# Attention: bias add, row statistics and reciprocals used at later steps, send casts chained to each other

## The chip, the cores and the metric

One NeuronCore of a Trainium2 chip runs the whole program. The metric is the device time of one execution in microseconds. One execution is also recorded by the hardware profiler; the times inside a profile are counted from the start of its span. TensorE (PE in the tables) multiplies matrices, VectorE (DVE), ScalarE (ACT) and GpSimd (POOL) do elementwise work, and SyncE (SP) issues most DMAs. Each engine works through its own queue in order.

## The reference

The network has two layers on an input x of shape 2 x 256 x 56 x 56 (batch, channels, height, width). The change lies in the first half of layer 0, local attention; the sends it speaks of feed the second half, a mixture of experts.

```python
# layer 0
x = x + L0_conv(ln_c(x))         # windowed attention, residual
t = to_tokens(x)
t = t + L0_ffn(ln_t(t))          # experts, top 2 of 8, residual
x = from_tokens(t, x)
# L0_conv: 8 heads of 32 channels, each query sees a 7 x 7 window
q, k, v = proj(x, wq, bq), proj(x, wk, bk), proj(x, wv, bv)
attn = softmax(einsum('bhdxy,bhdxyw->bhxyw', q, windows(k)) * scale)
out = proj(einsum('bhxyw,bhdxyw->bhdxy', attn, windows(v)), wo, bo)
# L0_ffn: logits = t @ router_w.T; softmax, top 2, weights normalised
out = t; for e in range(8): out += combine[:, e] * (gelu(t @ w1[e] + b1[e]) @ w2[e] + b2[e])
# layer 1: two ternary 3 x 3 convolutions with batch norm, then experts again
```

## The kernel before

**Strips and slots.** The image pair is cut into 14 strips of 8 rows (448 tokens, seven strips an image). The attention loop runs over the strips; each strip has 8 slots (4 windows of columns by 2 halves of the heads). In a slot, `scores` (L1485) computes the scores sc of one window on TensorE and their exponentials ex on ScalarE, and `attend` (L1518) takes the slot before: it multiplies ex by the values into av and adds av to the accumulator acc on VectorE (L1534). So in every slot 4 + 4 score products, 4 value products, 2 exponentials and 2 accumulations pass, and everything else of a strip is spread between them.

**Step by step helpers.** `project` and `leave` are generators: each `yield` ends a step. `project(g + 2)` runs one step a slot during strip g: row statistics of the input (`token_stats`, L709), the normalised rows xn on ScalarE (`scaled`, L735), their transposes (L1435), the k and q projections (L1447), the v projections (L1469). `leave(g - 1)` (L1539) begins once strip g's slots are written out, and `push` (L1618) advances each open generator one step a slot. Its steps in the kernel before:

1. `again` (L1376) loads the residual rows xr from memory on SP's queue (L1379) and adds the output bias bo to them (L1380) on GpSimd, or on VectorE for the last two strips; the sums of the softmax are stored (L1553) and come back as den (L1557).
2. nothing.
3. the reciprocal rden (L1560) is stored as shares (L1561) and comes back spread over partitions as rec (L1564); den is checked (L1570 to L1572).
4. nothing.
5. acc times rec gives oc (L1581), eight products on VectorE.
6. oc times wo gives pw on TensorE (L1594), added to xr (L1602).
7. `norm` (L766): row statistics of xr on VectorE (L714 to L719).
8. GpSimd turns them into t_rstd and t_nmr (L729 to L731); for the last two strips ScalarE and VectorE do it.
9. u, the normalised rows, on ScalarE (L737).
10. transposes of u (L784); u is added to xr (L791, GpSimd), which is stored as x_mid (L792).
11. the router's logits (L800, L811).
12. the strip is entered as routed.

When both strips of a pair are routed, `settle` (L814) follows: four steps find the top two experts and each token's place, and then comes one step for each of the 8 blocks of 112 tokens: a cast of the places to integers (L884, VectorE) and two sends, indirect DMAs from GpSimd that scatter rows of u to the experts' buffer xs (L888). The last two strips settle alone, 4 blocks each.

**Order.** In this stage a scheduler fixes each queue's order when the program is built: an instruction written earlier has precedence, but one that is ready in its model may pass others. `tc.issue_after(pace[-1])` (L883) keeps a cast behind the last accumulation of its slot; `attend` sets `pace` (L1537), and it is cleared after the loop (L1661). Inside the expert stage (`experts`, L1045) the order on SP, VectorE, TensorE and ScalarE is as written.

**End of the loop.** `plan_first` (L1626) plans the first 27 expert tiles as soon as strips 0 to 9 are counted (`FIRST`). After the loop the experts start: weights (L1097) and rows of xs (L1086) are loaded, rows are transposed (L1107), multiplied (L1139, L1158), and the results are scattered to ys from GpSimd (L1170). At each tile `beside` (L1730) pushes the leaves and settles that are still open; when none is left, `routed_all` (L1684) plans the other tiles and computes the gates, TensorE's product pf (L1695) among it.

Buffers: xr and xt have two each, oc and rec one, u four.

Of the kernel before, what the change touches and what calls it, by code (L numbers as in the profile page):

```python
# [66 lines left out]
FIRST = (10, 8)  # L67
# [13 lines left out]
def bcast(ap, axis, shape):  # L81
    return ap.unsqueeze(axis).to_broadcast(shape)
# [551 lines left out]
def metaformer(ctx: ExitStack, tc: tile.TileContext, a: dict, out: bass.AP, flag):  # L634
    nc = tc.nc
# [73 lines left out]
    def token_stats(tp, src, eps, root, paced=False):  # L709

        stats = tp.tile([TT, NTT, 6], F32, tag="t_stats", name="t_stats")
        mv = tp.tile([TT, NTT, 2], F32, tag="t_mv", name="t_mv", bufs=3)
        for t in range(NTT):
            nc.vector.bn_stats(stats[:, t, :], src[:, t, :])  # L714
        for t in range(NTT):
            nc.vector.bn_aggr(mv[:, t, :], stats[:, t, :])
        rstd = tp.tile([TT, NTT], F32, tag="t_rstd", name="t_rstd", bufs=3)
        nmr = tp.tile([TT, NTT], F32, tag="t_nmr", name="t_nmr", bufs=3)
        nc.vector.tensor_scalar_mul(nmr, mv[:, :, 0], -1.0)  # L719
        if paced:  # L720
            yield
        if root:
            nc.scalar.activation(rstd, mv[:, :, 1], AF.Sqrt, bias=eps[:TT])
        yield
        if root:
            nc.vector.reciprocal(rstd, rstd)
            nc.vector.tensor_tensor(nmr, nmr, rstd, ALU.mult)
        else:
            nc.gpsimd.tensor_tensor(rstd, mv[:, :, 1], eps[:TT].to_broadcast([TT, NTT]), ALU.add)  # L729
            nc.gpsimd.tensor_tensor(rstd, rstd, minus_half, ALU.pow)  # L730
            nc.gpsimd.tensor_tensor(nmr, nmr, rstd, ALU.mult)  # L731
            yield
        return rstd, nmr

    def scaled(dest, src, rstd, nmr):  # L735
# [9 lines left out]
    pace = []  # L745

    def routing(layer, wp, tp, ps):
# [66 lines left out]
        def settle(strips, paced=False):  # L814


            n = len(strips) * NTT
            t0 = strips[0] * NTT
            us = [rows.pop(i) for i in strips]
            full, row = [TT, n, E], (TT, n)  # L820

            def small(name, shape=(TT, n, E), dt=F32):
                return tp.tile(list(shape), dt, tag=f"{name}_{n}", name=name, bufs=1)

            def first_max(v, m, hot, at):

                nc.vector.tensor_reduce(m, v, AX.X, ALU.max)
                nc.vector.tensor_tensor(hot, v, bcast(m, 2, full), ALU.is_equal)
                nc.vector.tensor_tensor(hot, hot, bcast(order, 1, full), ALU.mult)
                nc.vector.tensor_reduce(at, hot, AX.X, ALU.min)  # L830
                nc.vector.tensor_tensor(
                    hot, bcast(order, 1, full), bcast(at, 2, full), ALU.is_equal
                )

            lg = lgs[:, t0 : t0 + n, :]
            m = [most[:, j, t0 : t0 + n] for j in range(TOP)]
            hot = small("hot", (TT, TOP, n, E))
            at = small("at", (TT, TOP, n))
            rest = small("rest")
            first_max(lg, m[0], hot[:, 0], at[:, 0])  # L840
            for q, u in enumerate(us):
                small_eng.tensor_copy(u[:, :, R_EX], at[:, 0, q * NTT : (q + 1) * NTT])
            nc.vector.scalar_tensor_tensor(rest, hot[:, 0], NEVER, lg, ALU.mult, ALU.add)
            yield
            first_max(rest, m[1], hot[:, 1], at[:, 1])
            yield

            hots = small("hots", dt=BF16)
            nc.vector.tensor_tensor(hots, hot[:, 0], hot[:, 1], ALU.add)
            seen_b = small("seen_b", (TT, E), BF16)  # L850
            nc.vector.tensor_copy(seen_b, seen)
            here = small("here", (TT, E))
            nc.vector.tensor_reduce(here, hots.rearrange("p n e -> p e n"), AX.X, ALU.add)
            nc.vector.tensor_tensor(seen, seen, here, ALU.add)
            if strips[-1] == FIRST[layer] - 1:
                nc.vector.tensor_copy(seen_b4, seen)
                counted.append(True)
            if paced:
                yield
            rk = ps.tile([TT, n, E], F32, tag="aux", name="rk")  # L860
            nc.tensor.matmul(rk, before_w, hots, start=True, stop=False)
            nc.tensor.matmul(rk, all_w[:, :TT], bcast(seen_b, 1, full), start=False, stop=n == 1)
            for t in range(n - 1):
                nc.tensor.matmul(
                    rk[:, t + 1 :, :],
                    all_w[:, :TT],
                    bcast(hots[:, t, :], 1, [TT, n - 1 - t, E]),
                    start=False,
                    stop=t == n - 2,
                )  # L870
            yield
            place = small("place")
            nc.vector.tensor_tensor(place, rk, bcast(base_t, 1, full), ALU.add)
            nc.vector.tensor_tensor(hot, hot, bcast(place, 1, [TT, TOP, n, E]), ALU.mult)
            rowf = small("rowf", (TT, TOP, n))
            nc.vector.tensor_reduce(rowf, hot, AX.X, ALU.add)
            if layer == 1:
                nc.vector.tensor_copy(pos[:, :, t0 : t0 + n], rowf)
            yield
            for t in range(n):  # L880
                if layer == 0:

                    with tc.issue_after(pace[-1]) if pace else nullcontext():  # L883
                        nc.vector.tensor_copy(  # L884
                            pos[:, :, t0 + t : t0 + t + 1], rowf[:, :, t : t + 1]
                        )
                for j in range(TOP):
                    w = nc.gpsimd.indirect_dma_start(  # L888
                        xs[:, :],
                        bass.IndirectOffsetOnAxis(ap=pos[:, j, t0 + t : t0 + t + 1], axis=0),  # L890
                        us[t // NTT][:, t % NTT, :],
                        None,
                    )
                    apart(f"rows{layer}", w)
                    if FIRST[layer] and strips[0] >= FIRST[layer]:

                        disjoint(w, f"late{layer}", f"early{layer}")
                yield
            sent.extend(strips)
# [453 lines left out]
    with ExitStack() as st:  # L1353
        aw = st.enter_context(tc.tile_pool(name="att_w", bufs=1, reuse_waits="tile"))
        tp = st.enter_context(tc.tile_pool(name="att_t", bufs=2, reuse_waits="tile"))
        ps = st.enter_context(tc.tile_pool(name="att_ps", bufs=2, space=PSUM, reuse_waits="tile"))
# [16 lines left out]
            xt[g] = sp.tile([TT, NTT, C], F32, tag="xt", name="xt")  # L1373
            nc.sync.dma_start(xt[g], a["x_tok"][g])

        def again(g, eng):  # L1376

            xr[g] = tp.tile([TT, NTT, C], F32, tag="xr", name="xr")
            nc.sync.dma_start(xr[g], a["x_tok"][g])  # L1379
            eng.tensor_tensor(xr[g], xr[g], bcast(bias["o"], 1, [TT, NTT, C]), ALU.add)  # L1380

        load(0)
# [37 lines left out]
            nc.gpsimd.memset(t[:, :, :, 1:3, :], 1.0)  # L1420
            vals.append(t)
        keys = {}
        norm0, settle0, tiles0, _, gates0, wgt0, counted0, _ = routing(0, aw, tp, ps)

        def project(g):
            s = g % NS
# [112 lines left out]
        def leave(g):  # L1539
# [2 lines left out]
            rows = slice(s * SR, (s + 1) * SR)  # L1542

            late = g >= len(STRIPS) - 2
            again(g, nc.vector if late else nc.gpsimd)


            sums = dram.tile([2, PAIRS * NT], F32, tag="sums", name="sums", bufs=2)
# [8 lines left out]
            nc.sync.dma_start(den, sums.rearrange("i (p n) -> (i p) n", n=DEN))  # L1557
            yield
            yield
            nc.vector.reciprocal(rden, den)  # L1560
            nc.sync.dma_start(shares.rearrange("i (p n) -> (i p) n", n=DEN), rden)  # L1561
            rec = tp.tile([P, PAIRS, NT], F32, tag="taken", name="rec", bufs=1)
# [7 lines left out]
            nc.vector.tensor_scalar(fit, den, LEAST, None, ALU.is_ge)  # L1570
            nc.vector.scalar_tensor_tensor(fit, den, MOST, fit, ALU.is_le, ALU.mult)
            nc.vector.tensor_tensor(fits, fits, fit, ALU.add)  # L1572
            yield
            yield
            oc = tp.tile([P, KC, NT], F32, tag="oc", name="oc", bufs=1)
# [48 lines left out]
        plans0, taken = [], []  # L1624

        def plan_first():  # L1626
            if counted0 and not plans0:
                plan, n = tiles0(0)
                plans0.append(plan)
                taken.append(n)  # L1630
# [7 lines left out]
        for g in range(len(STRIPS)):  # L1638
# [18 lines left out]
            if g % NS == NS - 1:  # L1657
                attend(*before)
                before = None
                under_way.append(later(4, leave(g)))  # L1660
        pace.clear()  # L1661
        loop.close()
        while not plans0:
            push()
            plan_first()


        tiles_on = ctx.enter_context(ExitStack())
# [81 lines left out]
    with mid:  # L1750

        with ExitStack() as st:
            rp = st.enter_context(tc.tile_pool(name="raw", bufs=1, reuse_waits="tile"))
            ps = st.enter_context(tc.tile_pool(name="conv_ps", bufs=4, space=PSUM, reuse_waits="tile"))
# [9 lines left out]
            tp = strips_on.enter_context(  # L1764
                tc.tile_pool(name="conv_t", bufs=2, side="right", reuse_waits="tile")
            )
# [320 lines left out]
        with ExitStack() as both:  # L2087
# [6 lines left out]
            tp = both.enter_context(  # L2094
                tc.tile_pool(name="route_t1", bufs=2, side="right", reuse_waits="tile")
            )
# [55 lines left out]
            norm, settle, tiles, planning, gates, wgt1, _, sent = routing(1, wp, tp, ps)  # L2152
# [259 lines left out]
```

## Time and profile before

| what | us |
|---|---|
| runs | 1847.08, 1842.25, 1848.16; median 1847.08 |
| the profiled execution, its own time | 1836.06 |
| its span | 1834.3 |
| attention, first accumulation to the last | 44.6 to 516.5 |
| first expert tile's transposes | 524.5 |
| last expert product of layer 0 | about 831 |

| engine | busy us | share of the span | instructions |
|---|---|---|---|
| TensorE, matmul | 1523.4 | 83% | 8612 |
| VectorE | 978.8 | 53% | 2690 |
| ScalarE | 701.5 | 38% | 1362 |
| GpSimd | 656.1 | 36% | 664 |

How to read it: a group of lines names line, engine, operation and tile, `out<-in`; a bracket at the end of a timeline row gives the idle time of the engine before that instruction and what ended it. `remote` and `issue` there mean that the profile shows no releaser. A matmul counts with its modelled end. The granted clock is the share of TensorE's full speed.

### The profile page before, as it was taken

To read this page: it belongs to the slowest core of one execution; us is meant where nothing else is said; L and a number is where in the kernel's file an instruction comes from. 1 tells how busy PE (TensorE), PEld (TensorE's weight loads), DVE (VectorE), ACT (ScalarE), POOL (GpSimd) and SP (SyncE) were. 2 spreads that over 40 slices of the span, in tenths; PEclk is the share of its full clock that TensorE was granted. 3 is DMA by queue.
4 is the path that set the end of the run, shared out by engine and by line. 5 is a ranking of instruction groups with operands and counts; after the bars stand their busy time and mean duration, and the time that the engine had idled before them with its cause. 6 is when DMAs were issued, how large, how long until landed. Compare 5 with 4: busy or idle time off the path is not lost. (4 is left out here: it accounts for less than half of the span.)

```text
span 1834.3 us, 25840 instructions
## 1 busy us (share of the span) xinstructions
PE 1523.4 (83%) x8612; PEld 1191.8 (65%) x8612; DVE 978.8 (53%) x2690; ACT 701.5 (38%) x1362; POOL 656.1 (36%) x664
## 2 busy tenths in 40 slices
PE   6999998899788858894899799666468799999964
PEld 3555565555466747782788687556457688988953
DVE  4467556476645336855999897675422211111137
ACT  3454433434333324643454443233243333333322
POOL 3012524335343663442244144154553322222210
PEclk9999988999888979996999899755579899999985
DMA  7022324212267757985652000033635568888858
GB/s 241 27 82 83 108 88 122 58 56 83 57 192 232 248 192 265 308 274 161 166 161 61 1 1 1 21 114 99 226 129 186 179 232 273 286 276 294 287 181 311
DMA packets 91886, 291.77 MB, mean 159 GB/s; under 512 B 20487, under 2 KB 35803, under 8 KB 80416
## 3 DMA queue, kind: packets, MB, share of 16 engines
q1 hardware_dynamic: 66736, 231.79, 39.8%
q0 software_dynamic: 21200, 51.82, 8.1%
q10 hardware_dynamic: 3808, 6.42, 1.0%
q8 instruction: 70, 1.15, 0.3%
q14 instruction: 72, 0.59, 0.1%
HBM read 218.51 MB, written 74.20 MB: 160 GB/s over the span
## 5 line engine op out<-in xcount | busy, mean ns | idle before, releaser
L1139 PE MATMUL ph<-ut,w 128*128 128x256 f32 (+1 forms) x1472 | 316.8, 366 | 32.7 <-ACT h L1146 27.5
L1158 PE MATMUL py<-w,h 128*128 128x256 f32 x1288 | 304.1, 385 | 0.0
L1139 PEld LDWEIGHTS ph<-ut,w 128*128 128x128 f32 x1472 | 255.1, 198 | 63.5 <-ACT h L1146 29.0
L1168 DVE TENSOR_TENSOR y<-py,w 128x512 f32<-128x512 f32 (+1 forms) x120 | 76.8, 640 | 409.6 <-PE py L1158 358.2
L888 POOL DMA_INDIRECT xs<-u,pos x224 | 218.1, 974 | 168.6 <-issue 84.4
L1158 PEld LDWEIGHTS py<-w,h 128*128 128x128 f32 x1288 | 247.4, 194 | 34.6 <-DVE y L1168 0.4
L1170 POOL DMA_INDIRECT ys<-y,dest x136 | 136.7, 1005 | 269.9 <-DVE dest L1114 161.0
L1146 ACT ACTIVATE h<-ph,w 128x256 f32<-128x256 f32 (+1 forms) x368 | 162.4, 448 | 115.6 <-PE ph L1139 84.4
L1514 ACT ACTIVATE ex<-sc 112x476 f32<-112x476 f32 (+3 forms) x224 | 117.0, 571 | 207.0 <-PE sc L1504 172.9
L1111 ACT COPY ut<-pt 128x512 f32<-128x512 f32 (+1 forms) x120 | 65.3, 544 | 320.0 <-PE pt L1107 234.2
L1524 PE MATMUL av<-ex,vals 112*64 112x238 f32 (+3 forms) x896 | 125.9, 403 | 16.2 <-DVE acc L1534 15.0
L1534 DVE TENSOR_TENSOR acc<-av,acc 128x238 f32<-128x238 f32 (+3 forms) x224 | 88.1, 408 | 95.4 <-PE av L1524 72.1
L1832 PE MATMUL pc<-lo,wq 128*128 128x448 f32 x336 | 131.5, 393 | 7.3 <-DVE lo L1807 7.2
L1832 PE MATMUL pc<-hi,wq 128*128 128x448 f32 x336 | 131.0, 392 | 3.2 <-DVE x L1856 3.0
L1170 POOL DMA_INDIRECT ys<-y,to x81 | 82.4, 1018 | 128.3 <-DVE dest L1114 74.7
L1975 PE MATMUL pc<-hi,wq 128*128 128x448 f32 (+1 forms) x288 | 102.8, 366 | 18.0 <-ACT hi L1942 9.4
L1229 DVE SCALAR_TENSOR_TENSOR x<-got,wgt,x 112x256 f32<-112x256 f32 x216 | 102.4, 546 | 28.1 <-DMA got<-ys 27.6
L1495 PE MATMUL sc<-q_im,keys 32*112 32x238 f32 (+3 forms) x896 | 95.6, 431 | 11.6 <-ACT ex L1514 7.4
L1975 PE MATMUL pc<-lo,wq 128*128 128x448 f32 (+1 forms) x288 | 101.8, 363 | 0.2 <-DVE lo L1943 0.2
L1524 PEld LDWEIGHTS av<-ex,vals 112*64 112x64 f32 x896 | 57.1, 143 | 66.1 <-issue 26.8
L1107 PE MATMUL pt<-ident,xg 128*128 128x128 f32 x434 | 72.4, 288 | 26.3 <-ACT ut L1111 21.0
L1805 POOL TENSOR_TENSOR v<-pad 128x928 f32<-128x928 f32 (+1 forms) x28 | 56.3, 2023 | 100.3 <-DVE lo L1807 49.1
(273 smaller groups left out, 2467.2 us busy)
## 6 DMA issues: line engine op xcount, KB each, us to landing
w<-in_L_experts SPq DMA_DIRECT2D x64, 1154.0 KB
w<-in_L_experts SPq DMA_DIRECT2D x56, 641.0 KB
xg<-xs SPq DMA_DIRECT2D x97, 260.0 KB
got<-ys SPq DMA_DIRECT2D x28, 896.0 KB
acc<-in_fresh SPq DMA_DIRECT2D x14, 896.0 KB
xt<-in_x_tok SPq DMA_DIRECT2D x14, 448.0 KB
xr<-in_x_tok SPq DMA_DIRECT2D x14, 448.0 KB
rec<-shares SPq DMA_DIRECT2D x28, 224.0 KB
```

What stands on the lines that cost most here:

```text
L888: w = nc.gpsimd.indirect_dma_start(xs[:, :], bass.IndirectOffsetOnAxis(ap=pos[:, j, t0 + t : t0 + t + 1], axis=0), us[t // NTT][:, t % NTT ...
L1139: nc.tensor.matmul(ph[:, :g], w1[:, k, f * P : (f + 1) * P], d["ut"][:, k, :g], start=k == 0, stop=k == KC - 1,)
L1146: nc.scalar.activation(d["h"][:, f, :g], ph[:, :g], AF.Gelu, bias=b1[:, f : f + 1])
L1158: nc.tensor.matmul(py[:, i, :], d["h"][:, f, i * P : (i + 1) * P], w2[:, f, :], start=f == 0, stop=f == NF - 1,)
L1170: o = nc.gpsimd.indirect_dma_start(ys[:, :], bass.IndirectOffsetOnAxis(ap=d["to"][:, i : i + 1], axis=0), y[:, i, :], None, bounds_check=T ...
L1229: nc.vector.scalar_tensor_tensor(xt[:, t, :], y[:, t, j, :], wgt[:, j, n : n + 1], xt[:, t, :], ALU.mult, ALU.add)
L1495: nc.tensor.matmul(sc[h // 2][:, h % 2, :nq], keys[g][p, c, tx * TT : (tx + 1) * TT], q_im[p, c, r0:r1, c0:c1], start=True, stop=False,)
L1514: nc.scalar.activation(e[:, :, :nq], sc[j][:, :, :nq], AF.Exp, scale=HD**-0.5)
L1524: nc.tensor.matmul(av[VW * i : VW * (i + 1), :nq], vals[g % 3][:, tx, 2 * c + j, 2 * i : 2 * i + 2, :].rearrange("p a d -> p (a d)"), ex[j ...
L1534: added = nc.vector.tensor_tensor(d, av[:, :nq].rearrange("p (h w) -> p h w", w=c1 - c0), d, ALU.add)
L1832: nc.tensor.matmul(pc[:, :NT], wq[:, k, c, dx * C + o * P : dx * C + (o + 1) * P], part[:, :, k, dx : dx + W], start=m == 0, stop=m == 2 * ...
L1975: nc.tensor.matmul(pc[:, : 2 * ns * W], wq[:, k, c, dx * C + o * P : dx * C + (o + 1) * P], part[:, : 2 * ns, k, dx : dx + W], start=m == ...
```

## The change

Four edits in the attention stage.

- `token_stats` yields once more after GpSimd's statistics, so their users come a step later, in `project` and in `leave` (not for the last two strips of `leave`, whose statistics take the other branch).
- `again` is split: it loads xr in step 1, and the bias add, now `biased`, stands in step 3, ahead of the reciprocal.
- One more `yield` stands between the reciprocal's step and the products oc.
- Each send cast becomes the last entry of `pace`, so that a cast follows the cast before it where no accumulation came between; `pace` is cleared later; and the loop after attention goes on until the sends of strip 9 have been written out.

```diff
@@ token_stats
             nc.gpsimd.tensor_tensor(nmr, nmr, rstd, ALU.mult)
             yield
+            yield
         return rstd, nmr
@@ settle
                     with tc.issue_after(pace[-1]) if pace else nullcontext():
-                        nc.vector.tensor_copy(
+                        cast = nc.vector.tensor_copy(
                             pos[:, :, t0 + t : t0 + t + 1], rowf[:, :, t : t + 1]
                         )
+                    if pace:
+                        pace[:] = [cast.ins]
@@ again
-        def again(g, eng):
+        def again(g):
             xr[g] = tp.tile([TT, NTT, C], F32, tag="xr", name="xr")
             nc.sync.dma_start(xr[g], a["x_tok"][g])
+
+        def biased(g, eng):
+
             eng.tensor_tensor(xr[g], xr[g], bcast(bias["o"], 1, [TT, NTT, C]), ALU.add)
@@
-        norm0, settle0, tiles0, _, gates0, wgt0, counted0, _ = routing(0, aw, tp, ps)
+        norm0, settle0, tiles0, _, gates0, wgt0, counted0, sent0 = routing(0, aw, tp, ps)
@@ leave
-            again(g, nc.vector if late else nc.gpsimd)
+            again(g)
...
             yield
             yield
+            biased(g, nc.vector if late else nc.gpsimd)
             nc.vector.reciprocal(rden, den)
...
             nc.vector.tensor_tensor(fits, fits, fit, ALU.add)
             yield
             yield
+            yield
             oc = tp.tile([P, KC, NT], F32, tag="oc", name="oc", bufs=1)
@@ after the loop
-        pace.clear()
         loop.close()
-        while not plans0:
+        while not plans0 or FIRST[0] - 1 not in sent0:
             push()
             plan_first()
+        pace.clear()
```

## The prediction

> **What bounds the kernel now.** I read the slices of the page first, then the chain of waits, then the stage that the change touches, strip by strip. The first two lines below are TensorE's busy tenths and granted clock in 40 slices of 45.9 us, the third the shares of the chain that ended last.
>
> ```profile
> PE   6999998899788858894899799666468799999964
> PEclk9999988999888979996999899755579899999985
> PE 22%; another core or an unknown queue 3%; issue 2%; DVE 2%; DMA 2%; ACT 1%; POOL 0%; ACTq 0%; DVEq 0%; POOLq 0%; SPq 0%
> ```
>
> The reader is to see that TensorE is busy nearly throughout the first eleven slices (attention, 0 to about 516 us), that its clock dips in slices 6, 7 and 11 to 13, and that the chain is too short (about a third of the span) to price anything here: followed in time it begins at 1241 us, long after the change. What the change is worth has to be read in the attention stage and at its end.
>
> So I cut that stage at the first accumulation (L1534) of each strip. Columns: bounds and length, then each engine's busy us (instructions), granted clock, DMA share, GB/s; strips 5 to 11.
>
> ```profile
> 191.50:229.90 38.40, 34.03 (x242) 20.32 (x240) 21.61 (x63) 15.80 (x31) 23.72 (x26) 0.92 0.40 120
> 229.90:266.90 37.00, 34.86 (x257) 22.38 (x253) 23.23 (x75) 14.37 (x32) 8.66 (x13) 0.89 0.22 67
> 266.90:310.10 43.20, 36.44 (x242) 22.12 (x239) 28.41 (x75) 14.77 (x31) 23.93 (x28) 0.83 0.45 132
> 310.10:354.30 44.20, 41.50 (x273) 25.45 (x271) 20.71 (x64) 16.40 (x32) 11.09 (x12) 0.89 0.20 63
> 354.30:389.60 35.30, 33.18 (x220) 18.14 (x216) 20.32 (x53) 14.99 (x29) 19.06 (x22) 0.95 0.26 75
> 389.60:423.80 34.20, 32.34 (x253) 19.59 (x249) 22.92 (x65) 15.64 (x31) 6.86 (x10) 1.00 0.16 49
> 423.80:457.50 33.70, 32.11 (x244) 19.05 (x240) 21.45 (x54) 14.28 (x27) 22.50 (x23) 1.00 0.30 93
> ```
>
> The last two strips are what a strip costs when TensorE runs through at full clock: 33.95 us on average. Strips 5 to 9 last 198.1 us against 5 x 33.95 = 169.75, an excess of 28.4. One leave more falls into them (the image boundary has two), worth on TensorE 3.71 (pw) + 0.99 (pu) + 1.74 (pl) = 6.4 us. The other 22.0 us are idle time and half clock. Who makes TensorE idle in these five strips, us in total, times, longest:
>
> ```profile
> PE sc L1495 <- ACT ex L1514: 5.8, 4, 2.6
> PE av L1524 <- DVE acc L1534: 4.8, 2, 3.1
> PE pw L1594 <- DVE q_im L1459: 3.9, 2, 2.1
> PE pw L1594 <- DVE oc L1581: 2.5, 1, 2.5
> PE pu L784 <- DVE q_im L1459: 1.0, 1, 1.0
> ```
>
> That is 18.0 us. One step behind these stand the waits which the change aims at (ScalarE, then VectorE, from the timelines):
>
> ```profile
> 222.01 2.07 ACT L737 ACTIVATE u<-xr,t_nmr,t_rstd 112x256 f32<-112x256 f32 x4 [5.46 <-POOL t_nmr L731]
> 260.87 1.09 ACT L737 ACTIVATE u<-xr,t_nmr,t_rstd 112x256 f32<-112x256 f32 x2 [11.00 <-POOL t_nmr L731]
> 245.36 2.31 DVE L1581 TENSOR_TENSOR oc<-acc,rec 32x448 f32<-32x448 f32 x4 [3.50 <-DMA rec<-shares]
> ```
>
> ScalarE stands 5.46 and 11.00 us at L737 for GpSimd's statistics, with the exponentials that TensorE needs queued behind it; VectorE stands 3.50 us for rec, with accumulations behind it.
>
> **The change part by part.** It adds and removes no instruction: the two builds hold the same ones on every engine, in another order, from the first strips to the end of attention. So every cost is a wait moved.
>
> *Residual load and bias add.* The load (L1379) keeps its place in SP's queue, directly behind the x_mid store, since its buffer is the limit. Only the add of 2.36 us (GpSimd, L1380) is written two steps later, and in the built order it hardly moves: ahead of a set of sends it still stands straight behind L791, waits 7 us and holds the first of them; in a strip with sends it stands near their end in both orders. GpSimd's idle time there (56.8 us in eleven waits up to 480 us) delays sends, and those have a whole strip of cover. I cost it at 0; without the cover it is the slower rival below.
>
> *Row statistics and reciprocals a step later.* In the built order u now comes after one more exponential pair, behind both v projections (2 x 1.98 us), and in strips 5, 9 and 11 ten sends of 1.25 us stand ahead of the statistics where twelve stood. In strip 6 three accumulations and the first top-2 search lie between reciprocal and oc, where two accumulations lay. That answers sc<-ex (5.8) and pw<-q_im (3.9), 9.7 of the 18.0 us, or 54%. Not pw<-oc at 293.8: the two oc bursts of the boundary stay within two slots. Nor av<-acc. I let the 22.0 us go with the idle time: 0.54 x 22.0 = 12 us gained. Bounds: 22 gained, and 10 lost if the waits return one slot later (two more gaps like those two at 5 us each, gap and half clock).
>
> Whether the clock comes back with the gaps is open. The row of the trace:
>
> ```profile
> 224.10:234.30 10.20, 9.71 (x68) 6.22 (x68) 1.60 (x5) 4.53 (x10) 5.38 (x7) 0.50 0.41 128
> ```
>
> The one gap near it is 2.56 us, ending at 224.59, and 10.2 us at 0.50 follow. [...]
>
> *Casts chained.* The send casts (L884, 0.16 us) stay one per slot inside the loop, as an accumulation resets the chain. 0. After the loop the last two casts follow the last accumulation.
>
> *The end of the loop.* All steps shift by two slots, so two of the eight pairs of sends of strips 8 and 9 fall behind the last accumulation, and the first expert rows must wait for them. Now:
>
> ```profile
> 515.25 0.94 POOL L888 DMA_INDIRECT xs<-u,pos  x1 [0.30 <-issue]
> 514.11 2.94 SPq L1097 DMA_DIRECT2D w<-in_L_experts  x3
> 521.60 4.82 SPq L1086 DMA_DIRECT2D xg<-xs  x5
> 524.48 1.11 PE L1107 MATMUL pt<-ident,xg 128*128 128x128 f32 x4 [2.63 <-DMA xg<-xs]
> ```
>
> The last send is issued at 515.25, xg at 521.60, the first expert transpose at 524.48, already waiting. Two pairs are 4 x 1.25 = 5.0 us, on the path: +5.0. In SP's queue sums, den and shares of leave(12) now stand between the weight loads and xg; shares wait for a reciprocal behind L1602 and the statistics (until about 524), which is earlier than the sends. Bounds 0 (nothing) and +8 (sends plus 3 us of that queue).
>
> *A bias add on VectorE.* leave(12) now starts before the experts, so its add (L1380 on VectorE, 1.22 us at 535.6 today) is built into strip 13, four slots from its end, with an accumulation behind it. Its load cannot leave before x_mid of strip 10 has landed (491.2 + 3), and took 7 us elsewhere: about 501 to 505 against 503 for that slot. +2.0; bounds 0 and 7 + 1.2 = 8.2.
>
> *Experts.* Three steps of the leaves run before the first tile instead of beside tiles, so one of two SP stalls at shares goes: TensorE's 3.45 us at 574.9. The late plan comes a tile earlier, but its 13.0 us for pf stay. -3.5; bounds -8 (both stalls, 3.45 + 4.92 at 555 to 559) and 0.
>
> Sum: -12 + 5 + 2 - 3.5 = -8.5 us. The profiled execution took 1836.06 us (span 1834.3 and 1.8 around it), which becomes 1827.6. It lies 11 us below the median of the runs, 1847.08; carried over to that, **1839 us**.
>
> **The rivals.**
>
> *The stalls only move* (nothing gained in the loop, end costs stay): 0 + 5 + 2 - 3.5 = +3.5, 1850.6. For it: the load still follows x_mid and GpSimd still waits for it ahead of the first sends in half the strips. Against: u stands later by more TensorE work than the statistics do. That the build does not do what the words say (the residual load begins no earlier, in strips 3 to 5 the reciprocal is built a slot later and oc in the same slot as now) ends here too.
>
> *GpSimd's queue becomes the wait* (slower). In strips with sends, the add behind its load, ten sends of 1.25 us, the drain before the memset (4.9 us at 208 to 213) and the statistics are one queue, and the first casts come two slots later. It decides where nmr lands after ScalarE reaches u. Strip 5 shows the price today: 38.4 - 33.95 = 4.5 us. If strips 9, 11 and 13 pay it too and strips 5 to 8 keep theirs: 3 x 4.5 = 13.5, + 5 + 2 - 3.5 = +17, 1864. With one strip alone +8, 1855. For it: GpSimd is busy 23.7 us in strip 5 besides its waits. Against: strip 11 has the same 16 sends and no loss.
>
> *All of the excess goes*: -22 + 5 + 2 - 3.5 = -18.5, 1828.6. For it: strips 10 and 11 show full clock is possible. Against: av<-acc is untouched.
>
> **How the numbers follow.** Forecast 0.45 (1832 to 1845), all of the excess 0.10, stalls only move 0.20, GpSimd's queue 0.25. A measurement of this kernel tells about 0.3%, 5.5 us, from no change: 1841.5 and 1852.6. Faster: most of the forecast (0.40) and 0.10, 0.50. Same: the rest of the forecast and most of the second case, 0.20. Slower: the third case and 0.05 of the second, 0.30. The range 1821 to 1860 takes in all but the far ends of the outer cases.
>
> **What would show it.** Right: strips 5 to 7 near 35 us with granted clock over 0.95, ACT's wait for t_nmr well under 10 us in 220 to 480 (now 22.7), expert rows issued some 11 us after the last accumulation (now 5). Wrong: a wait of L737 for t_nmr in strips 9 or 11, new half-clock stretches after 360 us, or a VectorE wait for xr near the end of strip 13 of more than 5 us.

## The result and the profile after

The changed kernel took 1845.57 us, median of 22 runs (1837.08 to 1859.61), the kernel before 1848.36 us, median of 22 runs on the same chip. The ratio is 0.9991, 95% interval 0.997 to 1.0011: no change that can be told from none. Two later comparisons gave 0.9985 (0.996 to 1.001) and 1.0005 (0.9982 to 1.0028). Forecast was 8 us faster.

The profiled execution took 1841.9 us (span 1840.1). First the slices and the shares of the chain that ended last:

```profile
PE   6999998999778668984899699665378799999953
PEclk9999998999889889996999899755589899999975
...
PE 23%; another core or an unknown queue 3%; issue 3%; DMA 2%; DVE 2%; ACT 2%; POOL 0%; ACTq 0%; POOLq 0%; DVEq 0%; SPq 0%
```

In attention (the first eleven slices) the clock still dips, in slices 7 and 11; before it was 6, 7 and 11. Strips 5 to 11, cut at the first accumulation as before; columns are bounds and length, each engine's busy us, granted clock, DMA share, GB/s:

```profile
195.02:229.63 34.61, 33.28 (x250) 20.20 (x250) 21.49 (x63) 16.03 (x32) 19.96 (x22) 1.00 0.40 121
229.63:265.77 36.14, 34.98 (x255) 22.03 (x251) 24.09 (x75) 14.40 (x30) 11.91 (x17) 0.91 0.31 92
265.77:307.16 41.39, 36.78 (x250) 22.03 (x246) 28.17 (x75) 14.61 (x30) 21.70 (x24) 0.88 0.43 124
307.16:350.50 43.34, 39.65 (x269) 24.09 (x261) 19.78 (x64) 16.31 (x32) 13.16 (x16) 0.88 0.27 77
350.50:381.14 30.64, 30.56 (x220) 17.55 (x216) 18.98 (x52) 14.74 (x30) 15.62 (x19) 1.00 0.23 63
381.14:416.69 35.55, 34.97 (x253) 20.73 (x249) 21.82 (x66) 15.93 (x31) 10.44 (x13) 0.95 0.19 55
416.69:452.68 35.99, 35.99 (x244) 21.40 (x240) 19.35 (x53) 14.10 (x28) 18.00 (x19) 0.91 0.27 79
```

Strips 5 to 9 last 186.1 us instead of 198.1, but 10 and 11 now have half clock and are 1.3 and 2.3 us longer; strips 3 and 4 are together 3.3 us longer. What TensorE waits for in 191 to 390 us:

```profile
PE sc L1501 <- ACT ex L1520: 6.0, 2, 3.5
PE pw L1602 <- DVE oc L1589: 1.9, 1, 1.9
PE pw L1602 <- DVE q_im L1465: 1.3, 1, 1.3
PE av L1530 <- DVE acc L1540: 1.2, 2, 0.9
```

With a last wait of 0.2 that is 10.6 us instead of 18.0. Of the two waits which the prediction called answered, the one for q's eviction fell (3.9 to 1.3), but the one for the exponentials is as it was (5.8); the one for the accumulation, which it called untouched, fell too (4.8 to 1.2). ScalarE's waits at u in 222 to 320 us:

```profile
224.92 2.08 ACT L738 ACTIVATE u<-xr,t_nmr,t_rstd 112x256 f32<-112x256 f32 x4 [2.26 <-POOL t_nmr L731]
260.55 2.08 ACT L738 ACTIVATE u<-xr,t_nmr,t_rstd 112x256 f32<-112x256 f32 x4 [2.38 <-POOL t_nmr L731]
300.41 2.08 ACT L738 ACTIVATE u<-xr,t_nmr,t_rstd 112x256 f32<-112x256 f32 x4 [12.70 <-POOL t_nmr L731]
317.45 0.60 ACT L738 ACTIVATE u<-xr,t_nmr,t_rstd 112x256 f32<-112x256 f32 x1 [8.75 <-POOL t_nmr L731]
```

In 220 to 480 us this wait adds up to 31.0 us against 22.7 before. And the end of the loop (GpSimd's last send, SyncE's first loads of expert rows, TensorE):

```profile
513.38 0.94 POOL L891 DMA_INDIRECT xs<-u,pos  x1 [0.30 <-issue]
518.40 1.47 SPq L1089 DMA_DIRECT2D xg<-xs  x2
521.57 2.64 SPq L1089 DMA_DIRECT2D xg<-xs  x3
521.10 1.12 PE L1110 MATMUL pt<-ident,xg 128*128 128x128 f32 x4 [9.98 <-DMA xg<-xs]
```

The last accumulation is at 506.9, the last send starts 6.5 us behind it, and TensorE stands 9.98 us for the rows.

I cut each profile at five events: first and last accumulation (the loop), first expert product ph, the moment when GpSimd's queue comes to its first sum of expert outputs into the residual (L1224 of the kernel before; it waits there, the sum itself runs later; called the first sum from here on), end. The profiled pair gives: loop 471.6 and 461.8; last accumulation to first product 11.0 and 18.0; first product to first sum 305.4 and 302.8. At the first sum the changed kernel is 4.9 us ahead, at the end 5.8 us behind; it loses this after 1170 us, where both kernels issue the same instructions in the same order. A single pair of profiles could not settle it.

### The profile page after: what moved, and what is told of

The parts are those of the page before. It is cut to its first block, busy times and chain, and to the rows that moved or that the text cites. A ratio compares the mean times of both kernels' runs of the same rounds, so it can differ in the third digit from the quotient of the medians.

```text
span 1840.1 us, 25845 instructions
## 1 busy us (share of the span) xinstructions
PE 1522.1 (83%) x8612; PEld 1190.3 (65%) x8612; DVE 967.7 (53%) x2690; ACT 701.1 (38%) x1362; POOL 655.6 (36%) x664
## 5 line engine op out<-in xcount | busy, mean ns | idle before, releaser
L1142 PEld LDWEIGHTS ph<-ut,w 128*128 128x128 f32 x1472 | 252.7, 196 | 67.2 <-ACT h L1149 34.4
L1110 PEld LDWEIGHTS pt<-ident,xg 128*128 128x128 f32 x434 | 56.4, 148 | 64.1 <-ACT ut L1114 26.1
```

The source lines that it names most:

```text
L1110: nc.tensor.transpose(pt[:, k, i * P : (i + 1) * P], d["xg"][:, i, k * P : (k + 1) * P], ident)
L1142: nc.tensor.matmul(ph[:, :g], w1[:, k, f * P : (f + 1) * P], d["ut"][:, k, :g], start=k == 0, stop=k == KC - 1,)
```

## The experiments

All of them ran on chips on which the kernel before takes 1746 to 1748 us, not the 1848 of the first comparison; so a ratio is against the kernel before on the same chip, and times from profiles are compared among these runs alone. "Half clock" is the time in the loop at granted clock 0.5, "waits" the sum of TensorE's waits there, "rows" the last accumulation to the first expert product, "experts" from there to the first sum. us:

| kernel | ratio (95%) | loop | half clock | waits | rows | experts |
|---|---|---|---|---|---|---|
| rep_before | 1.0003 (0.998 to 1.0027) | 453.7 | 41 | 29 | 13.7 | 287.4 |
| rep_after | 0.9985 (0.996 to 1.001) | 449.5 | 38 | 23 | 18.0 | 279.8 |
| rep_after2 | 1.0005 (0.9982 to 1.0028) | 464.7 | 84 | 20 | 17.2 | 288.2 |
| fix9 | 0.9993 (0.9969 to 1.0017) | 451.5 | 49 | 18 | 14.2 | 297.6 |
| tail9 | 0.9972 (0.9949 to 0.9995) | 457.7 | 56 | 28 | 17.9 | 281.6 |
| split_only | 0.9998 (0.9976 to 1.002) | 453.5 | 42 | 26 | 13.6 | 292.2 |
| recip_only | 0.9985 (0.9965 to 1.0005) | 451.5 | 33 | 29 | 13.6 | 294.0 |
| stats_only | 0.9946 (0.9923 to 0.9969) | 443.4 | 25 | 23 | 13.0 | 286.5 |
| rep_stats | 0.9941 (0.992 to 0.9962) | 446.7 | 35 | 21 | 13.3 | 285.9 |
| stats_all | 0.9924 (0.9896 to 0.9951) | 444.6 | 25 | 24 | 13.6 | 283.4 |
| pw_step | 1.0019 (1.0 to 1.0038) | 452.6 | 41 | 25 | 18.6 | 285.8 |
| push_first | 0.9968 (0.9947 to 0.9988) | 452.1 | 60 | 16 | 17.8 | 281.2 |
| fix9_push3 | 0.9983 (0.9965 to 1.0001) | 454.5 | 55 | 19 | 22.4 | 282.4 |
| fix9_l8 | 0.9967 (0.9946 to 0.9987) | 451.2 | 53 | 17 | 13.6 | 294.8 |
| stats_l8 | 0.9916 (0.9885 to 0.9947) | 433.8 | 19 | 17 | 13.8 | 291.3 |
| stats_all_l8 | 0.9871 (0.9837 to 0.9905) | 432.3 | 17 | 17 | 14.0 | 282.4 |

**Is the one profile typical?** rep_after and rep_after2 are the changed kernel, rep_before the kernel before, all unaltered.

> The changed kernel again, unaltered, for a second profile. Theory A (the change gains about 10 us in the attention loop and gives 7 back between the last accumulation and the first expert product; what the first profile lost after 1300 us is run-to-run scatter): first to last accumulation 462 +- 3 us, last accumulation to first expert product 17 to 19, first product of the second layer's experts to the end anywhere from 495 to 507. Theory B (the loss after 1300 us belongs to the change): that last stretch again 503 to 507. Theory C (the loop's gain was an accident of one profile): loop over 468. Ratio to before 0.997 to 1.001 in all of them.

> The kernel before again, unaltered, for a second profile. Theory A: loop 472 +- 3 us, last accumulation to first expert product 10 to 12, last stretch anywhere from 495 to 507. Theory B: last stretch 493 to 497 as in the first profile. Theory C: loop anywhere from 462 to 475. Ratio 1.000 within 0.3%.

> The changed kernel once more, unaltered. Its first profile on a chip of this speed was its fastest execution of twelve (1735.1 against a median of 1747.5). Theory N: this profile shows the loop at 450 to 458 us, 40 to 60 us of it at half clock, last accumulation to first expert product 17 to 19; ratio 0.997 to 1.001.

The last stretch of the expectations (first product of the second layer's experts to the end) was 470.8 and 469.4 us for the changed kernel, 473.3 for the one before: theory B falls, what the first profile lost there was scatter. But the loop of the changed kernel is anything from 449.5 to 464.7 us, so theory A's steady 10 us in the loop falls as well. The windows over the loop (kernel before, then rep_after2, same columns as above) show in what:

```profile
45.50:499.20 453.70, 424.87 (x3178) 254.68 (x3175) 279.64 (x803) 193.88 (x378) 160.90 (x186) 0.95 0.27 80
```

```profile
44.60:509.30 464.70, 445.08 (x3176) 265.48 (x3173) 277.67 (x802) 195.79 (x378) 159.40 (x183) 0.91 0.27 78
```

The changed kernel's TensorE is idle for 19.6 us instead of 28.8, and busy for 20 us longer with the same matmuls, at a granted clock of 0.91 instead of 0.95.

**The end of the loop.** fix9 leaves the two added steps of `leave` out from strip 9 on; tail9 has them only there (g >= 9). The step behind the statistics is conditioned alike, in `leave` alone.

```diff
             yield
             yield
-            yield
+            if g < 9:
+                yield
             oc = tp.tile(...)
```

> The changed kernel with the two added steps (statistics, oc) left out for strips 9 to 13, so that the sends of strips 8 and 9 keep their old slots and fall before the last accumulation. Theory A: loop 460 to 465 us, last accumulation to first expert product back to 10 to 12, ratio 0.993 to 0.996. Rival D (the sends are not the cause: the tail is longer because the loop ended earlier, and xg waits for something that keeps its own time): tail still 16 to 19, ratio 0.997 to 1.001.

> The complement: the two added steps only for strips 9 to 13, none for 0 to 8. Theory A: strips 0 to 9 as in the kernel before, loop 470 to 475 us, last accumulation to first expert product 16 to 19, ratio 1.002 to 1.004. Rival D: tail 10 to 12, ratio 1.000.

The sends are the cause of the longer way to the first product: 14.2 and 17.9 us (13.7 in rep_before, where 10 to 12 was expected), and TensorE's longest wait for xg there is 9.9 us in rep_after and 8.6 in tail9, against 6.5 in rep_before and 5.5 in fix9; rival D falls. But both ratios miss. With the sends early fix9 gains nothing, though its strips 5 to 9 took 178.7 us against 187.5; and tail9, with the sends late, is not slower. Its experts are 5.8 us shorter than in rep_before, but loop and way to the first product together 8.2 longer, so these parts do not explain it. The prize of theory A was not at the end.

**Which of the two steps.** In `leave`, stats_only has the step behind the statistics for strips 0 to 8 and none ahead of oc, recip_only the other way round, split_only neither. stats_all is the change without its step ahead of oc, the third part of the diff, which stats_only and split_only have too. The first two parts are those of recip_only and split_only (in stats_only i < 9 stands for the False of the second). All of them keep the split bias add, the chained casts and the loop's end condition; and they keep one thing more: `project` calls `token_stats` as well, and its added step stays in all of these kernels, in fix9 and tail9 too. No run takes it out.

```diff
             nc.gpsimd.tensor_tensor(nmr, nmr, rstd, ALU.mult)
             yield
-            yield
+            if extra:
+                yield
         return rstd, nmr
...
-            rstd, nmr = yield from token_stats(tp, src, eps5, layer == 1 or late, paced)
+            rstd, nmr = yield from token_stats(tp, src, eps5, layer == 1 or late, paced, False)
...
             yield
             yield
-            yield
+            if False:
+                yield
             oc = tp.tile(...)
```

> The bias add split off and the extra step behind GpSimd's row statistics for strips 0 to 8; no extra step ahead of oc. Strips 5 to 9 took 198.1 and 187.5 us in the two profiles of the kernel before, 186.0 and 177.4 in the two of the changed one; strips 3 and 4 66.5 and 69.8. Theory A1 (the wait of ScalarE for the statistics was what cost the five strips, as the prediction had it): 176 to 180 us on the second chip (a first chip: 185 to 189), strips 3 and 4 near 66.5. Rival A2 (it was rec ahead of oc): 186 to 189 here, no gain. Ratio 0.996 to 1.001 either way.

> The bias add split off and the extra step ahead of oc for strips 0 to 8; none behind the statistics. Theory A1: strips 5 to 9 as in the kernel before, 186 to 189 us on the second chip, strips 3 and 4 near 70 if the added step there is what made them longer. Rival A2: 176 to 180.

> The changed kernel without either added step: the bias add stands two steps behind its load, the casts are chained, the loop's end waits for the sends. Theory J (the bias add's place and the chaining are worth nothing, as the prediction had it; what stats_only gained, 0.9946, comes from the step behind the statistics): loop 452 to 460 us, TensorE at half clock for 38 to 60 us of it, ratio 0.998 to 1.002. Rival K (stats_only and recip_only, whose strips 5 to 9 took 178 and 179 us against 187.5, share only the split and the chaining, so these carry the gain): loop 443 to 449, ratio 0.993 to 0.997.

> stats_only again, unaltered. Theory J: loop 441 to 448 us with 20 to 35 us at half clock (the kernel before and the changed one had 38 to 63), ratio 0.993 to 0.997. Rival L (its 0.9946 was luck of seven timed runs): ratio 0.998 to 1.001.

> The step behind the statistics for every strip that has it (0 to 11), none ahead of oc: the change less its reciprocal step. Against stats_only the sends of strips 8 and 9 come one step later, one pair of them behind the last accumulation. Theory J: loop as stats_only, 441 to 448; last accumulation to first expert product 15 to 17 against 13; ratio 0.994 to 0.998. Rival M (it is not the oc step but any later step in strips 9 to 13 that takes the gain back): loop 448 to 456, ratio 0.998 to 1.001.

This is the turn of the study. Split, chaining and the step in `project` together: 0.9998, nothing. The statistics' step of `leave` on top of them: 0.9946, again 0.9941, and 0.9924 for all strips. The oc step on top of them: 0.9985, not to be told from nothing; added to the statistics' step it takes all of it back (fix9 0.9993 against stats_only; the changed kernel 0.9985 and 1.0005 against stats_all). Strips 5 to 9 alone would not have shown it: they took 178 to 180 us with either step, so that of A1 and A2 neither holds as put. In rep_after the loss lies in the others, in rep_after2 in both (its strips 5 to 9 took 188.4 us): strip 3 took 32.5 us in stats_all and 34.7 and 36.0 in the changed kernel, strip 11 32.5 and 36.0 and 34.4. Rivals K, L and M fall. The windows over the loop of split_only and stats_all, to be held against the two above:

```profile
45.10:498.60 453.50, 427.45 (x3176) 258.46 (x3173) 277.03 (x802) 195.03 (x378) 160.98 (x187) 0.95 0.27 81
45.80:490.40 444.60, 420.62 (x3176) 254.87 (x3173) 275.53 (x801) 194.35 (x378) 160.84 (x186) 0.97 0.28 83
```

**How the oc step costs.** Strip 3 on VectorE and TensorE in stats_all:

```profile
139.54 2.33 DVE L1591 TENSOR_TENSOR oc<-acc,rec 32x448 f32<-32x448 f32 x4
144.54 0.69 DVE L1612 TENSOR_TENSOR xr<-pw,xr 112x512 f32<-112x512 f32 x1
149.77 0.68 DVE L1466 TENSOR_SCALAR q_im<-pj,bq 128x448 f32<-128x448 f32 x1 [0.89 <-PE pj L1454]
...
142.52 3.71 PE L1604 MATMUL pw<-wo,oc 128*112 128x256 f32 x16
147.96 3.27 PE L1454 MATMUL pj<-xc,wq 128*128 128x448 f32 x8
```

and in rep_after:

```profile
138.80 0.61 DVE L1589 TENSOR_TENSOR oc<-acc,rec 32x448 f32<-32x448 f32 x1 [2.89 <-DMA rec<-shares]
140.06 4.11 DVE L1589 TENSOR_TENSOR oc<-acc,rec 32x448 f32<-32x448 f32 x7
144.20 1.41 DVE L714 BATCH_NORM_STATS2 t_stats<-xt 112x6 f32<-112x256 f32 x4
146.81 1.27 DVE L1465 TENSOR_SCALAR q_im<-pj,bq 128x448 f32<-128x448 f32 x2
...
142.51 3.27 PE L1453 MATMUL pj<-xc,wq 128*128 128x448 f32 x8
147.55 3.71 PE L1602 MATMUL pw<-wo,oc 128*112 128x256 f32 x16 [1.76 <-DVE q_im L1465]
```

In stats_all pw stands ahead of q's projection and starts without a wait. One slot later it stands behind that projection, and pw needs a buffer that VectorE frees only by evicting q (both tiles have the tag aux), with oc (4.7 us) and the statistics of xt (1.4) ahead of the eviction in VectorE's queue. TensorE stands 1.76 us. The order itself is not new. The kernel before has pw behind q as well, in strips 2 to 7 and 9 to 11; in strip 3 of rep_before it does not wait, as oc is done before q's product is:

```profile
136.60 4.66 DVE L1581 TENSOR_TENSOR oc<-acc,rec 32x448 f32<-32x448 f32 x8 [0.77 <-DMA rec<-shares]
142.35 0.67 DVE L1459 TENSOR_SCALAR q_im<-pj,bq 128x448 f32<-128x448 f32 x1
...
140.37 3.27 PE L1447 MATMUL pj<-xc,wq 128*128 128x448 f32 x8
143.49 3.62 PE L1594 MATMUL pw<-wo,oc 128*112 128x256 f32 x16
```

With the step in `project` the projections come later (in strip 3 the first product of k starts 9.4 us after the first accumulation in rep_before, 11.5 in split_only), and pw gets ahead of q; the oc step puts it behind again. Two kernels test what that costs. push_first keeps both steps of the change, but steps the leaves ahead of the next strip's projection in each turn of the loop; pw_step puts the second step behind oc.

```diff
-                    next(ahead, None)
                     push()
                     plan_first()
+                    next(ahead, None)
```

```diff
-            yield
             oc = tp.tile(...)
...
             yield
+            yield
             for t in range(0, NTT, 2):
                 pw = ps.tile(...)
```

> The changed kernel, both added steps kept, but in every turn of the loop the leaves are stepped ahead of the next strip's projection instead of behind it, so that the product pw and its sum stand again ahead of the eviction of q on TensorE and VectorE, while oc stays where the change put it. Theory N (the oc step takes the gain back because it puts pw behind the eviction of q, in front of which VectorE still has 4.7 us of oc): waits of pw for q_im near 0 (the changed kernel 2.3 and 4.8 us), strips 3 and 11 near 32.5 us (35 and 36), half clock in the loop 20 to 35 us (38 to 63), ratio 0.993 to 0.997. Rival P (it is the later oc itself, and all that follows it): strips 3 and 11 stay at 34 to 37, ratio 0.998 to 1.001.

> The changed kernel with the second added step put behind oc instead of ahead of it: oc stands in its old slot, pw one later, behind the eviction of q. Theory N: as the changed kernel, strips 3 and 11 at 34 to 37 us, ratio 0.997 to 1.001. Rival P: strips 3 and 11 near 32.5, ratio 0.993 to 0.996.

pw_step, with oc in its old slot and pw and all that follows it one slot later, is 1.0019: the later oc is not needed for the loss, and rival P falls as far as it speaks of oc. Its waits:

```profile
PE sc L1501 <- ACT ex L1520: 6.9, 3, 2.5
PE pw L1602 <- DVE q_im L1465: 6.5, 6, 2.0
PE pw L1602 <- DVE oc L1588: 4.8, 2, 3.8
```

push_first, with pw ahead of q again, has no such wait:

```profile
PE av L1530 <- DVE acc L1540: 4.5, 3, 3.5
PE pw L1602 <- DVE oc L1589: 3.7, 3, 2.2
PE sc L1501 <- ACT ex L1520: 3.0, 2, 1.8
```

Its 0.9968 is a gain (1742.08 us against 1749.36 for the changed kernel on the same chip), but about half of what stats_all has; strips 3 and 11 are at 33.6 and 34.4 us, between the two, and its half clock, 60 us, is not in the 20 to 35 expected (strips 7 and 8 took 87.5 us there). So it is shown that the order of the leaves' steps and the projection's matters. That it does so through pw's wait, as theory N has it, is not. The waits for q_im add up to 2.3 to 4.8 us in the changed kernel, where some 12 us are lost; recip_only has pw behind q too, with 3.8 us of these waits, and cannot be told from split_only, which has pw ahead (0.9985 and 0.9998). And strip 11 does not fit: in fix9 pw stands ahead of q there and TensorE waits for nothing, but the strip is as long as in rep_after, by half clock (stats_all, rep_after, fix9):

```profile
409.95:442.45 32.50, 32.50 (x244) 19.62 (x240) 21.12 (x54) 14.03 (x27) 19.95 (x21) 1.00 0.28 81
408.10:444.09 35.99, 35.99 (x244) 21.38 (x240) 19.96 (x54) 14.10 (x28) 18.18 (x19) 0.91 0.27 79
409.07:445.87 36.80, 36.80 (x244) 21.40 (x240) 19.07 (x54) 13.98 (x28) 18.01 (x19) 0.91 0.28 84
```

What the oc step takes back in the loop is half clock (25 us in stats_all, 38 and 84 in the changed kernel, with 24 us of waits against 23 and 20), and some 4 us more on the way to the first product (13.6 against 18.0 and 17.2). Why there is more half clock stays open. No run has two added steps in `leave` that both stand ahead of u, behind the statistics, so it is also open whether any second step would do.

**The experts.** fix9_push3 is fix9 with three more steps of the last leaves ahead of the first expert tile, as the changed kernel's longer end of the loop gives them.

```diff
             push()
             plan_first()
+        for _ in range(3):
+            push()
```

> As fix9 (no added steps from strip 9 on, so the sends fall before the last accumulation), and three further steps of the last leaves ahead of the first expert tile, as the changed kernel has them from its longer end of the loop. Theory E (what the changed kernel gained in the experts, 280 to 282 us against 287 to 298 from the first expert product to the first sum, comes from these three steps): last accumulation to first product 13 to 15, then 278 to 284, ratio 0.992 to 0.996. Rival F (the experts' time is scatter): anywhere from 278 to 298, ratio 0.997 to 1.002.

The experts become as short as theory E has it (282.4 against 297.6 in fix9), but the steps stand in front of the first product: 22.4 us instead of 14.2. More than half of the gain is paid there, and the ratio, 0.9983, is that of rival F.

**The image boundary.** What the runs pointed to beyond the change: in fix9_l8, stats_l8 and stats_all_l8 the second leave at the boundary begins eight slots after the turn, in the one strip in which no other leave starts.

```diff
-                under_way.append(later(4, leave(g)))
+                under_way.append(later(8 if g < NS else 4, leave(g)))
```

> As fix9, and the second leave at the image boundary (strip 6) begins eight slots after the loop's turn instead of four, so that it falls into strip 8, where no other leave starts. Theory G (strips 7 and 8 are long because two leaves fall together: they took 78.5 to 87.4 us in six profiles, where two strips with one leave take 68): 74 to 78 us, loop 4 to 8 us shorter than that of fix9 on the same chip, ratio 0.993 to 0.998. Rival H (the work is only moved): 79 to 84, ratio 0.999 to 1.002.

> stats_only with the second leave at the image boundary begun eight slots after the turn instead of four. With the oc step (fix9_l8 against fix9) strips 7 and 8 fell from 81.5 to 72.4 us and the ratio went from 0.9993 to 0.9967. Theory G (the same holds without the oc step): strips 7 and 8 72 to 75 against 81.1, ratio 0.989 to 0.993. Rival H (what is won there is lost in strips 9 to 13, which were 2.3 us longer in fix9_l8): ratio 0.994 to 0.997.

> The step behind the statistics for all strips, none ahead of oc, and the second leave at the image boundary begun eight slots after the turn: the best version that the runs point to. Theory G: strips 7 and 8 69 to 73 us, loop 432 to 438, ratio 0.988 to 0.992. Rival H (nothing beyond stats_all's 0.9924 and stats_l8's 0.9916): 0.991 to 0.994.

Strip 8 in stats_all, then in stats_all_l8:

```profile
296.83:342.18 45.35, 43.41 (x277) 26.60 (x273) 18.81 (x63) 16.15 (x32) 12.12 (x15) 0.84 0.20 65
```

```profile
293.98:329.02 35.04, 35.04 (x253) 20.91 (x249) 18.21 (x62) 15.35 (x30) 9.77 (x14) 0.93 0.26 82
```

Ten us shorter, with 24 matmuls fewer in it and the clock at 0.93 instead of 0.84, and strip 7 as long as before (35.8 in both): the work is done where it hides. fix9_l8 has the shorter strips 7 and 8 too (72.4 us against 81.5) but not the shorter loop of theory G, 451.2 against 451.5, though its ratio, 0.9967, lies in that theory's range: strips 9 to 13 were longer by 5.7. Without the oc step the gain stays: the loop is 433.8 us in stats_l8, whose ratio lies within theory G. stats_all_l8 is the fastest kernel of the study, 0.9871, beyond the 0.988 of theory G: 1724.8 us against 1748.0.

## Why the prediction was wrong, step by step

- **The yardstick of 33.95 us.** Strips 10 and 11 have full clock, but TensorE does not run through in them: it is idle for 1.86 and 1.59 us by the prediction's own rows.
- **Residual load and bias add, 0; casts chained, 0.** Right as far as it is shown: together with the step in `project` they give 0.9998 (split_only).
- **Row statistics and reciprocals a step later, -12.** This is the step that failed. I priced two edits as one, as "9.7 of the 18.0 us, or 54%". They do not add up to a gain. The statistics' step in `leave` is worth 0.54% to 0.76%, 9 to 13 us of 1746, without the oc step as much as I gave to both; the oc step without it nothing that can be told (0.9985). With both the ratio is 0.9994 (mean of three) instead of 0.9924, some 12 us back. The wait of pw for q_im, which I called answered, was a term to look at: the step in `project` had brought pw ahead of q, and waits for q_im are gone in split_only and stats_all; the oc step puts pw behind q again, and they are back (2.3 to 4.8 us in the changed kernel, 6.5 in pw_step; the kernel before had 7.0 and 1.9). How much of the 12 us they cost is not shown.
- **"I let the 22.0 us go with the idle time."** Wrong as well. TensorE's waits in the loop did fall, from 39 to 24 us in the first pair and from 29 to 23 and 20 later. The half clock did not follow: 60 to 63 us in the first pair, 41 against 38 and 84 later. The loop is long or short by its half clock: stats_all with 24 us of waits has 25 us of it, fix9 with 18 us has 49. The gain of the statistics' step is of this kind too: from split_only to stats_all the loop falls by 8.9 us, the waits by 2 and the half clock by 16. The first pair's loop, 9.8 us shorter where the sum had 10, was luck of the draw.
- **Two pairs of sends, +5.** Right: +3.5 and +4.3 (17.2 and 18.0 us against 13.7), +7.0 in the first pair, and the rows were issued 11.5 us after the last accumulation where I wrote 11.
- **The bias add on VectorE, +2.** Strips 12 and 13 together: 49.9 and 54.1 us against 49.9 and 50.5 in rep_before and split_only, 54.1 against 58.7 in the first pair; no size can be told from these. The wait for the load, which made up the term, did not come: the add stands at 497.50 in the first profile, 1.22 us long, without a wait.
- **Experts, -3.5.** Not contradicted: -2.6 in the first pair; 279.8 and 288.2 against 287.4 and 292.2 later, which is too much scatter to tell.
- **The markers.** Strip 5 had full clock at 34.6 us, strips 6 and 7 did not (36.1 and 41.4 us at 0.91 and 0.88); and a sign of being wrong came true, new half clock after 360 us (strips 10 and 11). "ACT's wait for t_nmr well under 10 us" was a bad sign: it rose to 31.0 us, and in 45 to 490 us, where it is 28.8 us in the kernel before and 37.4 in the changed one, stats_all, 0.8% faster, has 51.0. A long wait there does not make the kernel slow; TensorE's wait for ex fell all the same, from 6.5 us in split_only to 3.4 in stats_all.
- **The rivals.** "The stalls only move" is nearest in result (+3.5 us forecast, -2.8 between the medians, which is no change), but it came another way: one step's gain, undone by another step, not one stall shifted. GpSimd's queue did not become the wait: in strips 9 and 11 the wait at u is 1.6 us each.

## What to carry to other kernels

Price each moved step by itself and then together: where one edit holds two shifts, one may undo what the other gains, and only kernels with one of them tell. A step in a helper moves every caller of it; a kernel that takes the step out of one caller still has it in the other, as `project` here. When work moves by a slot, look on every engine at what it changes places with, shared PSUM buffers too: in strip 3 of rep_after the product that stands behind a projection waits 1.76 us for the eviction of that projection. Before believing a stage's difference in one pair of profiles, profile the same kernel again.

## What was not expected of the hardware

The same kernel took 1848 us on the first chip and 1746 to 1748 on the others. A third of the difference lies in one stretch: the routing between the layers, second layer's first transpose to its first expert product, took 160.5 us on the first chip and 125.6 in rep_before, at the same granted clock of 0.50 and with the same 90 us of TensorE work. ScalarE waits there 42.4 us at ut for something that the profile does not name, which is not among its longest waits in rep_before; why is open.

In rep_after2 the clock also falls where TensorE shows no gap. Strip 3 has a stretch at half clock from about 135.6 us on: eight value products take 2.14 us at 136.68 and 1.16 at 144.50. TensorE is busy throughout the window, and its mean granted clock is 0.91:

```profile
126.00:162.00 36.00, 36.00 (x246) 21.08 (x240) 20.27 (x55) 15.99 (x30) 7.55 (x8) 0.91 0.27 79
```

Another execution of the same order (rep_after, the same strip) has none: its granted clock is 1.00. The longest wait of TensorE in the loop of rep_after2 is 3.2 us, and 84 us of that loop are at half clock. In the first pair of profiles nine such stretches begin in the loop of the kernel before (three of 3.4 us, two of 6.8, four of 10.2) and thirteen in that of the changed one (eight of 3.4, four of 6.8, one of 10.2). What sets them stays open; with 17 to 84 us of them in a loop of 430 to 470 they decide more than the waits do.
